# Zero products ahead of a recurrence moved from its own banks to the bank of the part before it, and two steps moved in a hand-written tail

## The chip, the cores and the metric

The kernel runs on one core of a Trainium2 chip. The metric is device time in microseconds (us) for one execution of the whole program. The engines are named as in the profile: PE (TensorE matmul), PEld (TensorE weight load), DVE (VectorE), ACT (ScalarE), POOL (GpSimd) and SP (SyncE, which only issues transfers here). ACTq and SPq are the issuing sides of ACT and SP.

## The reference, cut to what matters

The input is four images of 128 channels and 64 by 64 points. Two layers follow each other.

```python
# layer 0: layer norm over channels, a 3x3 depthwise convolution, attention in 16x16 windows
# layer 1, on t = the 4096 points of an image as tokens of 128 channels:
t = t + linear_attention(layer_norm(t))        # running sums of k v^T along the tokens
t = t + ffn(layer_norm(t))
# ffn: a recurrence along the tokens
Wx = batch_norm(x @ W.T)                       # mean and variance over ALL tokens of all images
y  = sigmoid(Wx[:, s] + y @ V.T)               # one step after another, s = 0, 1, 2, ...
```

The batch norm needs a mean and a variance over every token, so no step of the recurrence can use its input before the last token's product with W has been measured.

## The kernel before, in words

**First part.** The images are cut into 16 bands (`n` = 0 to 15) of 16 rows, and each band into four windows and into two halves of 512 tokens. The order of all instructions of PE, DVE, ACT and POOL is the order in which the Python code emits them: `in_order()` (line 249) chains each engine's instructions. What is emitted when is written out by hand in tables of step names: `START` for the first band, `SLOT` and `LAYER1` for the bands between, and `TAIL` (lines 83 to 95) for the end. A name like `product.z` is a step and the half that it works on. In `TAIL`, `y` and `z` are the two halves of band 14, `a` and `c` the two halves of band 15, the last one. `check.63` belongs to the last window (number 63).

The steps of layer 1 that matter here, each with its lines:

- `keep` (790): four PE transposes of the half's result (L313), an ACT copy to `rs_o` (L793), and a store of `rs_o` to memory from ACT's queue (L795).
- `measure_last` (680): four `bn_stats` and four `bn_aggr` on DVE (L292, L294), then two small POOL operations (L296, L297) that make 1/deviation for each token.
- `send` (683) and `spread` (694): SP writes these 512 factors to memory (L685), and ACT's queue reads them back to all 128 partitions as `factors` (L696, 256 KB).
- `product` (802): the product with W on PE (L815, two passes), then on DVE a multiplication with `factors` into `wx` (L816) and `bn_stats` of it (L822). The very last half, `c`, has no `factors`: it is normed first (`norm_last`, L304, and `turn_last`, four transposes L313 and an ACT copy L692), multiplied with W (L806), measured (L807), and then all statistics are combined: `bn_aggr` (L808), POOL's 1/deviation `sc` (L809, L810), `shift` (L811), and a copy of the product to `wx` (L812).
- `check` (606 and `in_range`, 550): three DVE operations that test whether the denominators of the attention lie in a range (L606, L554, L555).

The first part ends with `fill(bank(), 6)` (line 987). `fill(bk, n)` (267) issues `n` products of a constant zero matrix, 128x512 in bf16, to a PSUM bank. They compute nothing that is used.

**Recurrence.** All PSUM banks of the first part are given back (`main.close()`), and new ones are taken: two sets of three, `z0` to `z2`, and one called `okp`. One zero product goes to each of the six `z` banks (line 1053) and two to `okp`. Then come three products of the identity with `mv`, `sc` and `shift0` (L1057), whose results nobody reads. They wait for the statistics. Then the steps run: 4096 tokens of an image are cut into 128 segments of 32, all segments step together, and 9 steps (`WARM - 1`) at the end of the segments give the start values for the 32 counted ones. With one ACT step ahead of them, that makes 41 rounds. In each round, for three groups of columns, DVE has put `sc * wx + shift` into a `z` bank (`seed`, L1037, one operation for two rounds), PE adds `V y` to it (L1102), and ACT applies the sigmoid (L1107). POOL adds the residual (L1129), and the results are stored. The first round has a seed for itself alone; rounds 1 and 2 share the next three.

```python
def fill(bk, n):
    for _ in range(n):
        nc.tensor.matmul(bk, zeros, zeros[:, :1].to_broadcast([P, 512]), start=True, stop=True)
```

Of the kernel before, what the change touches and what calls it, by code (L numbers as in the profile page):

```python
# [17 lines left out]
P = 128  # L18
# [70 lines left out]
    "attend1.z keep.y send.y output.c spread.y measure.c turn.a measure_last.z",  # L89
    "norm.c keys.a values.a product.y queries.a turn.c turn_keys.a queries.c",  # L90
    "keys.c keep.z scores.a scores.c accumulate.a send.z attend0.a spread.z",
    "attend1.a check.63 values.c turn_keys.c measure_last.a send.a accumulate.c attend0.c",
    "attend1.c measure_last.c norm_last.c keep.a product.z spread.a product.a keep.c",
    "turn_last.c product.c",
)
DGROUP = 4
TINY, HUGE = 1e-30, 1e30
# [17 lines left out]
def conv_attn_hybrid(ctx: ExitStack, tc: tile.TileContext, ins: dict, out: bass.AP):  # L115
    nc = tc.nc
# [10 lines left out]
    def loaded(name, shape, dt=F32, src=None, eng=None):  # L127
# [4 lines left out]
    ident = const.tile([P, P], F32, name="ident")  # L132
# [12 lines left out]
        fill=0.0,  # L145
# [85 lines left out]
    for i in range(2):  # L231
        t = const.tile([P, 4, P + 1], F32, name=f"v1_{i}")
# [8 lines left out]
    shift0 = const.tile([P, 1], F32, name="shift0")  # L241
    beta0 = const.tile([P, 1], F32, name="beta0")
    mv = const.tile([P, 2], F32, name="mv")
    sc = const.tile([P, 1], F32, name="sc")
# [4 lines left out]
    def in_order():  # L249

        before = {}
        for ins in nc.cur_bb.bb.instructions[first:]:
            if ins.engine in ENGINES:
                if ins.engine in before:
                    tc.add_manual_dep(
                        ins,
                        before[ins.engine],
                        mybir.DependencyInfo(
                            mybir.DependencyClass.NoSync, mybir.DependencyReason.DATA
                        ),  # L260
                        reason="in order",
                    )
                before[ins.engine] = ins.name
# [3 lines left out]
    def fill(bk, n):  # L267

        for _ in range(n):
            nc.tensor.matmul(  # L270
                bk, zeros, zeros[:, :1].to_broadcast([P, 512]), start=True, stop=True
            )

    def bank():
        bk = ps.tile([P, 512], F32, tag="bank", name="bank")
        fill(bk, busy[0])
        busy[0] = 0
        return bk
# [569 lines left out]
    def do(what, which):  # L848
        name, at = what.split(".")
        if name == "warm":  # L850
            busy[0] += int(at)
            return
        h = which.get(at)
        if h is not None and name not in h.done:
            does[name](h)
            h.done.add(name)
# [125 lines left out]
    for what in " ".join(TAIL).split():  # L982
        if what.partition(".")[2].isdigit():
            block(what)
        else:
            do(what, which)
    fill(bank(), 6)
    in_order()
    main.close()

# [61 lines left out]
        for g in range(len(GROUPS)):  # L1052
            fill(ps_r.tile([P, 512], F32, tag=f"z{g}", name=f"z{g}"), 1)
    okp = ps_m.tile([P, 512], F32, tag="bank", name="bank")
    fill(okp, 2)
    for t in (mv[:, :1], sc, shift0):
        nc.tensor.matmul(  # L1057
            okp[:, :256], ident, t.to_broadcast([P, 256]), start=True, stop=True
        )


    warm = sp.tile([P, B, SEGS + 1], F32, name="warm")
    nc.gpsimd.memset(warm[:, :, 0:1], 0.0)

# [777 lines left out]
```

## Time and profile before

| what | value |
|---|---|
| median of 3 runs | 824.96 us (824.9 to 827.38) |
| the profiled execution's own time | 824.4 us |
| its span, first to last instruction | 822.6 us |
| mean granted TensorE clock over the span | 0.991 |
| PE busy | 795.0 us, 97% |
| DVE busy | 694.0 us, 84% |
| ACT busy | 530.2 us, 64% |
| POOL busy | 252.4 us, 31% |

The profiled execution lies 0.56 us under the median of the runs. Between its span and its time there are 1.8 us outside the instructions. Busy shares are averages over the whole program; the change touches only the stretch from about 749 us to 769 us, the seam between the two parts, so that stretch has to be read on its own: in order of time, with the wait that ends last before each step.

### The profile page before, as it was taken

What the parts mean: (1) busy time and instruction counts of PE and PEld (TensorE: products, weight loads), DVE (VectorE), ACT (ScalarE), POOL (GpSimd) and SP (SyncE); (2) the same over time, 40 slices, a digit from 0 to 9 for tenths busy, and PEclk for the clock granted to TensorE, in tenths of its full rate; (3) what the DMA queues carried; (4) which work ended last, traced back from release to release, by engine and by line L of the source; (5) the groups of instructions that cost most, each with busy time, mean ns of one, the idle gap of its engine ahead of it and who ended that gap; (6) DMA issues with size and microseconds to landing.
All of it is one profiled execution on the core that took longest, in us unless ns stands there. A gap on an engine that the chain in (4) does not pass through costs nothing.

```text
span 822.6 us, 28912 instructions
## 1 busy us (share of the span) xinstructions
PE 795.0 (97%) x11808; PEld 638.0 (78%) x11808; DVE 694.0 (84%) x2141; ACT 530.2 (64%) x1024; POOL 252.4 (31%) x362
## 2 busy tenths in 40 slices
PE   9999999999999999999999999999999999988893
PEld 6667878878787878788787878787887878766793
DVE  6657989998989898898979898998989896497885
ACT  4776566666767675766667676757666675622683
POOL 3023233413242332423132423323231312121193
PEclk9999999999999999999999999999999999999997
DMA  5122231414132232314132222323131312212796
GB/s 144 40 67 70 65 99 31 118 41 114 47 80 76 69 94 61 101 38 115 42 103 57 76 81 63 98 65 96 44 108 43 107 36 83 57 27 65 236 227 183
DMA packets 81430, 69.31 MB, mean 84 GB/s; under 512 B 44680, under 2 KB 63752, under 8 KB 81288
## 3 DMA queue, kind: packets, MB, share of 16 engines
q1 hardware_dynamic: 54072, 44.55, 19.1%
q10 hardware_dynamic: 26208, 19.15, 8.4%
q0 software_dynamic: 1008, 3.67, 2.6%
q8 instruction: 95, 1.56, 0.8%
q14 instruction: 47, 0.39, 0.2%
HBM read 40.03 MB, written 17.87 MB: 70 GB/s over the span
## 4 chain that ended last, share of the span: by engine, by line
PE 87%; DVE 6%; DMA 3%; POOL 1%; ACT 1%; issue 1%; SPq 0%; ACTq 0%; DVEq 0%; POOLq 0%
PE bank L483 13%; PE bank L536 7%; PE bank L565 7%; PE bank L654 7%; PE bank L701 7%; PE bank L496 6%; PE bank L580 6%; PE bank L313 5%; PE z L1102 5%; PE bank L717 3%; PE bank L738 3%; PE bank L815 3%; PE bank L755 3%; PE bank L774 3%; PE bank L776 3%; PE bank L523 3%
## 5 line engine op out<-in xcount | busy, mean ns | idle before, releaser
L421 DVE SCALAR_TENSOR_TENSOR y<-ypad,cpe_w,y 128x512 f32<-128x512 f32 x240 | 184.6, 769 | 12.1 <-ACT y L419 7.6
L545 ACT ACTIVATE es<-bank 128x512 f32<-128x512 f32 x256 | 132.2, 603 | 33.5 <-PE bank L536 33.5
L296 POOL TENSOR_SCALAR rs<-mv 128x4 f32<-128x4 f32 (+2 forms) x99 | 25.3, 256 | 371.4 <-DVE mv L294 369.7
L628 POOL TENSOR_TENSOR oT<-o_sb,rden 128x512 f32<-128x512 f32 x63 | 81.3, 1290 | 114.5 <-DMA rden<-rd 85.6
L297 POOL TENSOR_TENSOR rs<-rs,mhalf 128x4 f32<-128x4 f32 (+2 forms) x99 | 105.3, 1064 | 8.3
L580 PEld LDWEIGHTS bank<-es,v_sb 128*32 128x32 f32 x3072 | 63.2, 110 | 36.7 <-issue 32.2
L491 ACT COPY k<-bank 128x512 f32<-128x512 f32 x64 | 38.6, 603 | 64.3 <-PE bank L483 64.3
L536 PEld LDWEIGHTS bank<-q,k 32*64 32x64 f32 x4096 | 75.4, 130 | 2.7
L536 PE MATMUL bank<-q,k 32*64 32x96 f32 (+1 forms) x4096 | 77.5, 274 | 0.0
L565 PE MATMUL bank<-es,ones 128*32 128x512 f32 x512 | 71.2, 605 | 0.0
L580 PE MATMUL bank<-es,v_sb 128*32 128x96 f32 (+1 forms) x3072 | 70.0, 237 | 0.0
L654 PEld LDWEIGHTS bank<-woT,oT 128*128 128x128 f32 x512 | 59.5, 192 | 12.3 <-POOL oT L628 8.5
L483 PE MATMUL bank<-y2w,wqT 128*128 128x256 f32 x256 | 66.2, 381 | 0.0
L568 ACT COPY den<-bank 128x512 f32<-128x512 f32 x64 | 37.3, 583 | 44.7 <-PE bank L565 42.4
L483 PE MATMUL bank<-y2w,wkT 128*128 128x256 f32 x256 | 66.1, 381 | 0.0
L496 PE MATMUL bank<-wvT,y2w 128*128 128x256 f32 x256 | 65.9, 380 | 0.0
L701 PE MATMUL bank<-xl,awT 128*128 128x512 f32 x128 | 63.2, 594 | 1.8 <-ACT xl L678 1.8
L654 PE MATMUL bank<-woT,oT 128*128 128x128 f32 x512 | 60.6, 276 | 4.5 <-POOL oT L628 4.5
L703 ACT ACTIVATE low<-bank,minus 128x512 f32<-128x512 f32 x64 | 44.0, 687 | 22.4 <-PE bank L701 20.9
L292 DVE BATCH_NORM_STATS2 st<-x 128x6 f32<-128x128 f32 x256 | 55.4, 279 | 0.6
L496 PEld LDWEIGHTS bank<-wvT,y2w 128*128 128x128 f32 x256 | 48.5, 190 | 7.5 <-DVE y L421 0.8
L611 DVE TENSOR_TENSOR dc<-dc,pad_c 128x32 f32<-128x32 f32 x63 | 22.3, 353 | 37.5 <-DMA dc<-den 37.2
(151 smaller groups left out, 1673.2 us busy)
## 6 DMA issues: line engine op xcount, KB each, us to landing
rden<-rd SPq DMA_DIRECT2D x63, 256.0 KB
v_sb<-v_sb SPq DMA_DIRECT2D x128, 64.0 KB
factors<-factors ACTq DMA_DIRECT2D x31, 256.0 KB
xin<-in_xt SPq DMA_DIRECT2D x15, 512.0 KB
out<-rs_o ACTq DMA_DIRECT2D x16, 256.0 KB
resd<-rs_o ACTq DMA_DIRECT2D x16, 256.0 KB
out<-ot SPq DMA_DIRECT2D x32, 128.0 KB
out<-ys POOLq DMA_DIRECT2D x7, 512.0 KB, 6.9
```

Of the source, the lines that this page charges most:

```text
L292: nc.vector.bn_stats(st[:, j, :], piece)
L297: nc.gpsimd.tensor_tensor(rs[:, :n], rs[:, :n], mhalf[:, :n], ALU.pow)
L421: nc.vector.scalar_tensor_tensor(y2, src, cpe_w[:, tap : tap + 1], y2, ALU.mult, ALU.add)
L483: nc.tensor.matmul(pps[:, br * WT : (br + 1) * WT], wT[:, br * P : (br + 1) * P], y2, start=True, stop=True,)
L496: nc.tensor.matmul(vps[:, e * 256 : (e + 1) * 256], y2[:, e * P : (e + 1) * P], wvT, start=True, stop=True,)
L536: nc.tensor.matmul(sps[h][half * KC : (half + 1) * KC, cols], w["k"][rows, k0 : k0 + KC], w["q"][rows, cols], start=False, stop=br == BR - ...
L545: nc.scalar.activation(es, sps[h], AF.Exp, scale=scale)
L565: nc.tensor.matmul(dps[rows], ones[:, :HD], w["es", h], start=True, stop=True)
L580: nc.tensor.matmul(ops[rows, cols], w["v"][:, n, c0 : c0 + HD], w["es", h][:, cols], start=(br, n) == pieces[0], stop=(br, n) == pieces[-1],)
L628: nc.gpsimd.tensor_tensor(oTs[n][:, :, :, wj * WS : (wj + 1) * WS], w["o"].rearrange("p (a r c) -> p a r c", a=BR, c=WS), w["rden"].rearra ...
L654: nc.tensor.matmul(yps[:, j * P : (j + 1) * P], oT[:, br, t], woT[:, br, :], start=br == 0, stop=br == BR - 1,)
L701: nc.tensor.matmul(zps, awT[:, m * P : (m + 1) * P], h.xl, start=True, stop=True)
```

## The change

The zero products at the end of the first part go from 6 to 20. The two zero products to `okp` and the three products of the identity are dropped, the six to the `z` banks stay. In the tail, `check.63` goes from behind `attend1.a` to a place just ahead of `product.c`, and `product.z` goes from behind `keep.a` to a place ahead of `norm_last.c` and `keep.a`. On PE, `product.z` so stands ahead of the four transposes of `keep.a`; on DVE it stands ahead of the four L304 of `norm_last.c`. The order of the transfers on SP's and ACT's queues is as before.

```diff
     "attend1.z keep.y send.y output.c spread.y measure.c turn.a measure_last.z",
     "norm.c keys.a values.a product.y queries.a turn.c turn_keys.a queries.c",
     "keys.c keep.z scores.a scores.c accumulate.a send.z attend0.a spread.z",
-    "attend1.a check.63 values.c turn_keys.c measure_last.a send.a accumulate.c attend0.c",
-    "attend1.c measure_last.c norm_last.c keep.a product.z spread.a product.a keep.c",
-    "turn_last.c product.c",
+    "attend1.a values.c turn_keys.c measure_last.a send.a accumulate.c attend0.c attend1.c",
+    "measure_last.c product.z norm_last.c keep.a spread.a product.a keep.c turn_last.c",
+    "check.63 product.c",
 )
...
-    fill(bank(), 6)
+    fill(bank(), 20)
     in_order()
     main.close()
...
     okp = ps_m.tile([P, 512], F32, tag="bank", name="bank")
-    fill(okp, 2)
-    for t in (mv[:, :1], sc, shift0):
-        nc.tensor.matmul(
-            okp[:, :256], ident, t.to_broadcast([P, 256]), start=True, stop=True
-        )
```

## The prediction

> **What bounds the kernel now.** I read the clock row of the page first, then the chain of waits in order of time, then the seam in short stretches, then the instructions in order of time. PE is busy for 97% of the span, but around 764 us the chain passes through products that compute nothing:
>
> ```profile
> 760.53 0.69 DVE stats L822
> 761.22 0.61 DVE stats L807
> 761.83 0.02 issue
> 761.85 1.03 DVE mv L808
> ...
> 763.06 0.61 DVE wx L812
> 763.67 0.05 issue
> 763.72 2.34 PE z L270 x6
> 766.06 0.85 PE bank L270 x2
> 766.91 1.69 PE bank L1057 x6
> 768.61 38.79 PE z L1102 x242
> ```
>
> Columns: start, length, what. DVE leads up to 763.67, the statistics of the last half. Then eleven products without use fill PE until the recurrence. The next view has busy time by engine in two stretches; the third number from the end is PE's granted clock:
>
> ```profile
> 761.40:763.70 2.30, 0.00 (x0) 0.00 (x0) 2.19 (x4) 1.49 (x2) 0.65 (x2) 1.00 0.59 181
> 764.20:767.60 3.40, 3.40 (x10) 1.76 (x9) 3.05 (x8) 1.37 (x3) 0.00 (x0) 0.50 1.06 354
> ```
>
> PE is idle for 2.3 us, waiting for L812, and then has half its clock for 3.4 us. In order of time the recurrence's other needs are there sooner:
>
> ```profile
> 755.20 0.33 ACTq L696 DMA_DIRECT2D factors<-factors  x1
> 756.78 1.11 DVE L304 TENSOR_SCALAR xn<-x,mv,rs 128x128 f32<-128x128 f32 x4 [1.41 <-POOL rs L297]
> ...
> 759.48 1.01 DVE L816 TENSOR_TENSOR wx<-bank,factors 128x512 f32<-128x512 f32 x1
> 759.92 1.47 PE L270 MATMUL bank<-zeros 128*128 128x512 bf16 x6
> ...
> 764.28 1.37 ACT L1079 ACTIVATE ys<-wx,shift,sc 128x176 f32<-128x176 f32 x3 [0.59 <-DVE shift L1018]
> 764.64 2.78 DVE L1037 TENSOR_SCALAR z<-wx,sc,shift 128x176 f32<-128x176 f32 x6
> 768.45 3.81 PE L1102 MATMUL z<-ys,fvT 128*128 128x176 f32 x23
> ```
>
> The first `ys` exists at about 764.8 and the first seed at 765.1; the first L1102 runs at 768.45. So 3.3 us of PE's queue lie bare. Before that, DVE's only pause is the 1.41 us at 756.78.
>
> [...]
>
> **The change part by part**, in the times of the profiled execution.
>
> *check.63 leaves its place.* It costs 0.69 us on DVE (749.37 to 750.06 in the chain). `measure_last.a` and so `send.a` come 0.69 earlier. The next DVE step (L763) needs PE's L755, which starts only at 750.31, and L784 at 752.41 follows PE's L776; so `measure_last.c` still ends at 755.4. Gain there: about 0. What hides it is PE, and it leaves 0.6 us of DVE idle.
>
> *product.z goes first.* On DVE its L816 and L822 (1.05 and 0.63 to the next start) run in the pause: 755.40 to 757.08 instead of waiting until 756.78. L304 starts 0.3 late, at 757.08, and with it `turn_last`, L806 and the first zero product (759.92 to 760.22). L304 would free DVE at 758.16.
>
> On PE its two passes (0.43 each) now delay the transposes of `keep.a` from 753.10 to 753.96. Behind these stand, on ACT's queue, the copy L793 (753.74 to 754.60), the store L795 (754.35 to 755.21) and, 0.35 later, the broadcast L696: issue at 755.56 instead of 755.20. Before, L696 waited for `send.a`; that now lands 0.69 sooner and no longer decides.
>
> *The broadcast is late next.* How long it takes must be bounded. That of `z` was issued at 744.51, 0.42 behind a store, and the DMA share falls to 0 at 748.25: 3.7 us, and a completion some tenths later. That of `a`, 0.85 behind a store, had its data by 759.0, at most 3.8. Now it follows its store by 0.35. I take 4.0 to the wait's end (3.5 to 4.6): 759.6 (759.1 to 760.2). DVE is free at 758.16, so `product.a` waits 1.4 us, a new wait, and starts 0.15 later than before (759.48).
>
> Queued behind it on DVE: `check.63` (0.69, no longer hidden), then L807. So L807 goes from 761.14 to 759.63 + 1.66 + 0.69 = 762.0, that is 0.86 later. L808, `sc`, `shift0` and L812 follow: L812 ends at 764.53. The `res` loads on SP, ACT and POOL's memset, which waited for the last L816, now wait for `check.63` (about 1.5 us later). ACT then issues two loads and the table load, some 3.2 us as before, and is ready for L1079 at 765.3. The loads ended at 776 (DMA share) and would now end near 777.5; POOL's first read of `res`, at 779.10 before and near 777.5 then, needs only the first half of them, so I cost this at nothing.
>
> *20 zero products, not 6.* They run from 760.22 every 0.218 us, to 764.58, and bridge the idle 2.3 us. The clock stays full[...]. The six `z` products follow L812 without a gap, until 765.9 instead of 766.06.
>
> *Five products dropped.* Off the path: 0.85 + 1.69 = 2.54 us at the clock that they had.
>
> *The recurrence.* Seeds start at 764.64 + 0.86 = 765.50; `z` bank 0 is ready by then. The first is seen by PE about 0.5 later, so L1102 starts at 766.1. But the six seeds take 2.78 us, to 768.28; round 1's last group needs the sixth. Before, it ran 1.56 us after the first L1102 (770.01 against 768.45). 768.40 - 1.56 = 766.84 is where the recurrence effectively starts. The rounds, 38.8 us, and the end stay as they are.
>
> **Sum:** 768.45 - 766.84 = 1.6 us less. The profiled execution gives 824.4 - 1.6 = 822.8; the median shown stands 0.56 above it, so 824.96 - 1.6 = **823.4 us**, 0.19% less. About 0.3% (2.5 us) is what a measurement of this kernel can tell from no change, so I call this no change.
>
> **Rivals.**
>
> *Faster: broadcast in time, seeds hidden.* If the broadcast lands by 759.0, L807 is 0.2 later, and seeds allow 766.2; if the sixth seed costs nothing, PE's own queue sets 765.9. 768.45 - 765.9 = 2.55, so 822.4; a few tenths less where the runs have further half-clock windows. For it: other broadcasts ended within 3.8 us. Against: six seeds back to back on DVE.
>
> *No half clock before.* [...]in some executions the old seam may keep its clock. Its eleven products then end near 766.8 and the change gains -0.1: 825.0. Against: the profiled run has the half clock and is the quickest of the times shown.
>
> *Slower: the broadcast waits behind stores.* `check.63` and L807 stand behind it. Each 0.1 us of lateness costs 0.1. Break-even is a landing at 761.2, 5.6 us after issue; at 764 the time is 827.8. For it: the stores of `keep.a` and `keep.c` move 0.86 and 0.75 later[...]. Against: no such time to landing in the trace.
>
> *The clock falls anyway.* If a half-clock window meets the 20 products, they end up to 1.7 later (824.9). Against: the longest pauses ahead of them are 0.7 each.
>
> **Numbers.** No change 0.58 (my sum 0.40, no half clock 0.12, clock falls 0.06), faster by over 0.3% 0.33, slower by over 0.3% 0.09. The likeliest case alone, with the bounds of the broadcast, is 822.8 to 824.0. The range for 8 in 10 reaches into the faster and the unthrottled case: 821.6 to 825.4.
>
> **What would show it.** Right: clock 1.00 from 755 to 768; L807 near 762.0 with DVE idle ahead of L816 on a DMA; six `z` products without a pause; L1102 near 766.1 with waits for DVE in round 1. Wrong: L816 of `product.a` straight behind L304; PE idle ahead of the `z` products; a half-clock stretch; or the recurrence longer than 39.5 us.

## The result, and the profile after

The changed kernel was timed against the kernel before twice, each time with runs of both in one comparison. The medians were 825.2 us (22 runs) against 825.52 us (22 runs), a ratio of 0.9998 with a 95% interval of 0.9986 to 1.001; and, with the variants below, 824.55 us (22 runs) against 824.81 us (67 runs), a ratio of 0.9981, interval 0.9967 to 0.9996. The mean of the two ratios is 0.9990, or 0.9 us of 825; the two intervals allow 0.1 to 1.6 us for that mean when their errors are taken as independent (half widths 0.0012 and 0.0015, together 0.0009). By the bound of 0.3% that is no change, as forecast. Single runs of one kernel lie up to 8 us apart (820.12 to 828.07 for the kernel before), so that every statement on a microsecond needs many runs.

The profiled execution took 823.65 us, its span 821.9 us. To compare traces I measure one stretch in each: from the first L755 of `accumulate.c` (750.31 before, 751.84 after) to the first sigmoid of the recurrence's third round. I call it the **seam**. It took 20.57 us before and takes **18.57 us** after. From there to the start of PE's last product the two traces have 37.74 and 37.75 us. The profile after took only 0.75 us less, because its seam starts 1.5 us later; ahead of the seam it has a stretch at half clock, from 63.15 to 66.57 us, which the profile before has not.

The lines of the recurrence stand 7 lower than before: L1095 is the old L1102. This is the chain of waits after, in order of time (start, length, what):

```profile
756.90 0.93 DVE wx L816
...
757.86 0.69 DVE stats L822
758.55 0.26 DVE xn L304
...
759.98 0.59 ACT xl L692
...
760.62 1.12 PE bank L806 x2
761.75 0.22 PE bank L270
...
762.02 4.09 PE bank L270 x18
...
766.16 1.46 PE z L270 x6
767.62 0.87 PE z L1095 x6
```

Before, this chain ran on DVE from 756.78 on, over both L816 and the statistics, to the end of L812 at 763.67. Now it leaves DVE with L304 and stays on PE but for one copy: L806, the zero products in the old bank, the zero products in the `z` banks, the recurrence. The path through the statistics has vanished from it. In order of time, with each wait in brackets:

```profile
757.15 0.39 ACTq L696 DMA_DIRECT2D factors<-factors  x1
...
760.33 1.04 DVE L816 TENSOR_TENSOR wx<-bank,factors 128x512 f32<-128x512 f32 x1 [0.77 <-DMA factors<-factors]
...
762.70 0.69 DVE L807 BATCH_NORM_STATS2 stats<-bank 128x6 f32<-128x512 f32 x1
...
764.55 0.68 DVE L812 COPY wx<-bank 128x512 f32<-128x512 f32 x1
...
766.63 4.94 DVE L1037 TENSOR_SCALAR z<-wx,sc,shift 128x176 f32<-128x176 f32 x10 [0.55 <-PE z L270]
767.46 3.73 PE L1095 MATMUL z<-ys,fvT 128*128 128x176 f32 x19
```

Two waits are new. `product.a` waits 0.77 us for the broadcast, as forecast. And the first seed (L1037) waits 0.55 us for the zero product in its `z` bank, where it started 0.14 us behind the operation ahead of it before: L812 ends at 765.23, but PE reaches the `z` banks only at 766.16, 0.93 later. At the 0.218 us from one to the next that this trace shows, twenty zero products are too many by about four. Busy time by engine in two stretches (third number from the end: granted clock):

```profile
759.50:766.10 6.60, 5.87 (x23) 2.48 (x24) 5.39 (x14) 2.19 (x4) 0.86 (x3) 1.00 0.35 104
766.20:767.60 1.40, 1.40 (x7) 0.77 (x7) 0.97 (x3) 1.04 (x3) 0.00 (x0) 1.00 1.05 367
```

The clock is full and PE has no pause of 2.3 us. So the profile shows 2.0 us gone, and the timed runs only about half of that. The experiments ask which edit brought what, what bounds the new seam, and where the rest went.

### The profile page after: what moved, and what is told of

The parts are those of the page before. It is cut to its first block, busy times and chain, and to the rows that moved or that the text cites. A ratio compares the mean times of both kernels' runs of the same rounds, so it can differ in the third digit from the quotient of the medians.

```text
span 821.9 us, 28920 instructions
## 1 busy us (share of the span) xinstructions
PE 796.2 (97%) x11811; PEld 638.9 (78%) x11814; DVE 698.0 (85%) x2141; ACT 530.2 (65%) x1024; POOL 253.2 (31%) x362
## 4 chain that ended last, share of the span: by engine, by line
PE 93%; DVE 3%; ACT 1%; DMA 1%; POOL 1%; issue 0%; SPq 0%; DVEq 0%; POOLq 0%
PE bank L483 14%; PE bank L565 8%; PE bank L536 8%; PE bank L654 7%; PE bank L580 7%; PE bank L496 7%; PE bank L701 7%; PE bank L313 6%; PE z L1095 5%; PE bank L717 3%; PE bank L755 3%; PE bank L774 3%; PE bank L738 3%; PE bank L776 3%; PE bank L815 3%; PE bank L523 3%
## 5 line engine op out<-in xcount | busy, mean ns | idle before, releaser
L580 PEld LDWEIGHTS bank<-es,v_sb 128*32 128x32 f32 x3072 | 63.2, 110 | 36.7 <-issue 32.2
L654 PEld LDWEIGHTS bank<-woT,oT 128*128 128x128 f32 x512 | 61.2, 196 | 12.2 <-POOL oT L628 8.5
L654 PE MATMUL bank<-woT,oT 128*128 128x128 f32 x512 | 62.2, 280 | 4.5 <-POOL oT L628 4.5
L701 PE MATMUL bank<-xl,awT 128*128 128x512 f32 x128 | 63.2, 594 | 2.0 <-ACT xl L678 2.0
L611 DVE TENSOR_TENSOR dc<-dc,pad_c 128x32 f32<-128x32 f32 x63 | 25.5, 405 | 33.3 <-DMA dc<-den 33.2
```

What stands on the lines that cost most here:

```text
L580: nc.tensor.matmul(ops[rows, cols], w["v"][:, n, c0 : c0 + HD], w["es", h][:, cols], start=(br, n) == pieces[0], stop=(br, n) == pieces[-1],)
L654: nc.tensor.matmul(yps[:, j * P : (j + 1) * P], oT[:, br, t], woT[:, br, :], start=br == 0, stop=br == BR - 1,)
L701: nc.tensor.matmul(zps, awT[:, m * P : (m + 1) * P], h.xl, start=True, stop=True)
```

## Experiments

Theory A was the profile's: the seam is 2.0 us shorter in every run. Its rivals came as the results did: B, the added products or the moved tail eat the gain; C, the half clock does not meet the old seam in every run; D, PE's 20 products bind the new seam, and DVE does not. All kernels were timed in rounds beside the kernel before.

| kernel | seam in its profile, us | half clock in the seam, us after its start | ratio to before | 95% interval |
|---|---|---|---|---|
| before | 20.57 | 13.9 | | |
| before, again (e1) | 20.59 | 14.6 | 0.9997 | 0.9983 to 1.0012 |
| five products dropped (e2) | 18.11 | 8.1 | 0.9970 | 0.9958 to 0.9981 |
| 20 zero products (e3) | 19.67 | none | 0.9994 | 0.9976 to 1.0012 |
| tail moved (e4) | 20.61 | 14.7 | 0.9989 | 0.9977 to 1.0001 |
| changed kernel | 18.57 | none | 0.9998 | 0.9986 to 1.001 |
| changed kernel, again (e8) | 18.58 | none | 0.9981 | 0.9967 to 0.9996 |
| e2 and 20 products (e9) | 20.05 | 8.6 | 0.9988 | 0.9973 to 1.0004 |
| e2 and the tail (e10) | 18.39 | 9.0 | 0.9992 | 0.9974 to 1.001 |
| e2, new order, 13 products (e6) | 17.47 | none | 0.9968 | 0.9954 to 0.9983 |
| no zero product (e7) | 21.17 | 11.2, for 6.83 us | 1.0019 | 1.0005 to 1.0032 |
| 10 zero products (e11) | 18.90 | none | 0.9993 | 0.9979 to 1.0008 |
| changed, check.63 back (e12) | 18.57 | none | 0.9991 | 0.9978 to 1.0005 |
| changed, 14 products (e13) | 18.95 | 9.1 | 0.9987 | 0.9972 to 1.0002 |

**The three edits one by one.** e1 is the unchanged kernel.

> The kernel before, unchanged, timed against itself. Seam here means: from the start of the last L755 (accumulate.c) to the start of the third round's first sigmoid. In the profile before it was 770.89 - 750.31 = 20.6 us with a half-clock stretch inside, after it 770.41 - 751.84 = 18.6 without. My theory (the gain is there where the seam of before has its half clock, and the half-clock stretches elsewhere scatter the times): the seam is 20.6 if its idle 2.3 us meets a half clock and about 18.9 (20.6 - 1.7) if not, and the comparison with itself has a scatter of some 1 us in the median, which is as much as the gain looked for. Rival (the change has a loss of its own that eats a steady 2 us gain): the seam is 20.6 in each execution and the times of equal kernels agree within 0.1%.

Measured: 0.9997, and the seam repeats to 0.02 us. This is what the comparison cannot tell apart.

e2 drops only the five products:

```diff
-    fill(okp, 2)
-    for t in (mv[:, :1], sc, shift0):
-        nc.tensor.matmul(
-            okp[:, :256], ident, t.to_broadcast([P, 256]), start=True, stop=True
-        )
```

> Only the five products without use ahead of the recurrence are dropped; 6 zero products and the old tail. My theory: the seeds then bound the start, 764.64 + 3.78 = 768.4 for the third round's first sigmoid, so a seam of 18.1 at full clock and up to 18.8 with the half-clock stretch: 0.8 to 1.8 us less than before, nearly all that the whole change brings. Rival (the 20 zero products bring the gain by the clock): the seam stays near 20 us.

Measured: 0.9970, 2.5 us less, more than the whole change gives. The chain of waits of e2 (its L1097 is the old L1102), and busy time in its half clock:

```profile
764.46 0.61 DVE wx L812
765.12 1.48 PE z L270 x6
766.60 0.96 PE z L1097 x4
```

```profile
759.85:763.15 3.30, 2.58 (x4) 1.04 (x6) 3.23 (x5) 0.45 (x1) 0.10 (x1) 0.50 0.04 14
```

A half clock does meet this seam, at 8.1 us. But PE has only six zero products there and then waits for L812 anyway, so they take the wait's time and the seam is 18.11 all the same.

e3 changes only the count, e4 only the order of the tail (both as in the diff above):

```diff
-    fill(bank(), 6)
+    fill(bank(), 20)
```

> Only the zero products at the end of the first part go from 6 to 20; the five products and the old tail stay. My theory: full clock, the six z products from 764.3, the five others until 767.3, so a seam of 19.5 in every execution: 1.1 less than a before with half clock and 0.6 more than one without; no difference in the median within 1 us. Rival (the clock is the gain): 1.7 us less in the median.

> Only the tail is moved as in the change; 6 zero products and the five others stay. My theory: the pause at L304 that product.z fills is paid back by the later broadcast and by check.63 behind it, L807 stands 10.9 us after L755 as in both profiles (761.14 - 750.31 = 10.8, 762.70 - 751.84 = 10.9), the seam is 20.6 with the half clock or 18.9 without, no difference. Rival (a loss in the tail eats the gain of the rest): L807 comes 0.5 us or more later, and the time is 1 to 2 us longer.

Measured: e3 keeps its clock and has a seam of 19.67, 0.9 less than before; in time, 0.9994. e4 leaves the seam as it was (20.61), and its L807 stands 10.84 us after the seam's start, 10.83 before: what `product.z` gives in DVE's pause, `check.63` takes back. Its 0.9989 has an interval that reaches to no change, and nothing in the seam stands behind it. So, of the three edits, the dropping alone makes the seam shorter than the changed kernel has it.

**The changed kernel again, and in pairs of edits.**

> The changed kernel once more, timed against the kernel before beside its own variants. The stretch from the start of accumulate.c's L755 to the third round's first sigmoid was 20.57 us before and 18.57 after in the two profiles, and the dropping of five products alone gave 2.5 us of time. Theory A (the 2.0 us of the stretch are real in the timed runs; the first comparison, 0.17 us with an interval of 1 us to either side, met them with half-clock windows elsewhere): about 823.4, a ratio of 0.9975. Theory B (the moved tail and the 20 products cost in the timed runs what the dropped products give, by a half clock that the profile happened to miss): 825.2, a ratio of 1.000, and a half clock or a later L1095 in the stretch of this profile.

Measured: seam 18.58, time 0.9981: the ratio of theory A lies within this interval, and its seam is as in the first profile. Theory B's later L1095 is not there. With the first comparison, though, A's 2.0 us are not reached.

e9 is e2 with 20 zero products, e10 is e2 with the moved tail.

> Five products dropped and 20 zero products, the tail as before. By the prediction's steps the moved tail costs 0.86 us (check.63 uncovered ahead of L807): without it the zero products run from 759.92 to 764.28, L812 ends at 763.67, the sixth seed 0.86 earlier, so the stretch is 18.57 - 0.86 = 17.7 us if seeds bind, 18.1 if PE's 26 products bind. Theory A (the profile's: L807 stood at 10.86 after, 10.83 before, so the tail costs nothing): 18.1 to 18.5, no half clock in the stretch, time 822.9 to 823.4. Theory B (the tail is what eats the gain): 822.5 or less, at least 1.5 us below the changed kernel beside it.

> Five products dropped and the tail moved, 6 zero products as before. Theory A: PE is idle from 761.7 to about 764.5, 2.8 us, so most runs have the half clock over the six z products and the first round: the stretch is 18.6 us where the window misses it, 19.5 to 20.3 where it meets it; time 823.4 to 824.6. Theory B (the 20 products eat the gain): as fast as the dropping alone, 823.1.

Both profiles caught the early half clock. e9's busy time in it, and its chain:

```profile
763.10:766.40 3.30, 3.03 (x5) 1.20 (x7) 3.23 (x5) 0.00 (x0) 0.10 (x1) 0.50 0.00 0
```

```profile
765.87 4.39 PE bank L270 x18
770.30 1.46 PE z L270 x6
```

In order of time, e9's last copy of the statistics:

```profile
767.17 0.68 DVE L812 COPY wx<-bank 128x512 f32<-128x512 f32 x1
```

L806 (2.07 us, 1.12 in the changed kernel) and the first zero products run at half clock, the 20 start late and still run, and PE comes to the `z` banks at 770.30, 2.45 us after L812 has ended (767.85). The seam is 20.05, where I had expected 18.1 to 18.5. In e10, with six zero products, the same half clock (at 9.0 us) costs little: seam 18.39, with L812 0.24 later than in the changed kernel and 0.28 later than in e2. So the added products turn a half clock that cost nothing into one that costs up to 2 us (20.05 against the 18.11 of e2, one profile each). That is theory B's mechanism, in some executions. The times do not show it: e9 and e10 cannot be told from the changed kernel, and e10, without added products, is no nearer to e2 than e9. Its median, 823.9 us, lies where theory A had it (823.4 to 824.6), not at B's 823.1, but its interval reaches both.

**What binds the new seam.** e12 puts `check.63` back behind `attend1.a` and changes nothing else; e13 cuts the zero products of the changed kernel from 20 to 14.

> The changed kernel with check.63 back behind attend1.a alone (product.z stays first, 20 zero products). By the prediction's steps check.63 costs 0.69 behind product.a and nothing at its old place: L807 at 10.2 us after accumulate.c's L755 (10.86 after), L812 at 12.0. Theory D (in the changed kernel PE's 20 zero products bind, to 14.3, since the second seed there waited 0.55 for a z product): L1095 still at 15.6, the third round at 18.4 to 18.57, no gain from DVE's 0.69. Theory of the prediction (DVE's statistics and seeds bind): 17.9.

> The changed kernel with 14 zero products instead of 20. Theory D (PE's zero products bind and the seeds wait for the z products): 14 end at 12.8, L812 at 13.4, z products 13.45 to 14.8, first L1095 at 14.9, the third round at first seed + 3.88 = 18.16, 0.4 less than after; the pause is 0.6 us, no half clock; time 0.4 us less than the changed kernel. Theory of the prediction (20 products end with L812, so that fewer of them give nothing): 18.57 as after.

In e12, L807 stands at 10.37 instead of 10.86 us (0.49 earlier; `product.a` waits longer for its broadcast), L812 0.50 earlier, and the seam is 18.57, unchanged. In order of time:

```profile
765.28 0.68 DVE L812 COPY wx<-bank 128x512 f32<-128x512 f32 x1
...
767.39 1.46 PE L270 MATMUL z<-zeros 128*128 128x512 bf16 x6
767.87 3.33 DVE L1037 TENSOR_SCALAR z<-wx,sc,shift 128x176 f32<-128x176 f32 x7 [1.06 <-PE z L270]
```

All that DVE gained is waited away at the first seed: 1.06 us for its `z` bank, 0.55 in the changed kernel. (The expectation calls it the second seed.) Theory D is shown: PE's zero products bind, because they hold up the first seed. e13 did not give its answer: the early half clock met it at 9.1 us, its 14 products ended at 766.1, and the seam was 18.95, not 18.16. The 18.16 was not seen in a profile; the time (0.9987) agrees with it and with 18.57.

e6 frees both: five products dropped, 13 zero products, and this order.

```diff
-    "attend1.a values.c turn_keys.c measure_last.a send.a accumulate.c attend0.c attend1.c",
-    "measure_last.c product.z norm_last.c keep.a spread.a product.a keep.c turn_last.c",
-    "check.63 product.c",
+    "attend1.a check.63 values.c turn_keys.c measure_last.a send.a accumulate.c attend0.c",
+    "attend1.c measure_last.c keep.a product.z norm_last.c spread.a product.a keep.c",
+    "turn_last.c product.c",
-    fill(bank(), 20)
+    fill(bank(), 13)
```

> Five products dropped, 13 zero products, check.63 back behind attend1.a (hidden by PE there), and product.z in DVE's pause but behind keep.a's transposes, so that the broadcast isn't late. By the prediction's steps this keeps the 0.74 us that product.z's place gives and loses none: L807 at 10.1 us after accumulate.c's L755 (10.83 before, 10.86 after), L812 at 11.95, seeds from 13.5, PE's z products from about 12.1 to 13.4; the stretch 17.8 us at full clock, 0.7 less than after. Theory A: 822.7. Rival: PE decides, not DVE (keep.a's transposes ahead of product.z delay L816 or the first zero product), and the stretch is 18.5 as after.

Measured: L807 at 10.19, seam 17.47, 0.3 less than expected, and 0.9968 in time, the best of all, level with e2. Only the broadcast came late all the same: it was issued 4.80 us after the seam's start, and `product.a` waited for it until 8.51. Its chain of waits, and the start of its seeds in order of time:

```profile
762.35 2.57 PE bank L270 x11
...
764.96 1.46 PE z L270 x6
766.42 0.95 PE z L1095 x4
...
767.40 0.33 ACT ys L1100
```

```profile
765.50 0.22 DVE L1019 SCALAR_TENSOR_TENSOR shift<-shift,sc,beta 128x1 f32<-128x1 f32 x1
...
765.85 5.49 DVE L1037 TENSOR_SCALAR z<-wx,sc,shift 128x176 f32<-128x176 f32 x11
```

The first seed follows L1019 without a wait for a `z` bank: the products no longer hold it up. From the start of the first seed to the third round it is 3.77 or 3.78 us in all eight profiles of kernels with the five products dropped: e6 (13.69 to 17.47), e2 (14.34 to 18.11) and e10 (14.62 to 18.39), where the seed does not wait, but also the changed kernel (14.79 to 18.57). So DVE's six seeds set this last stretch in each, and zero products cost what they delay the first seed by. In the changed kernel DVE was ready for it at about 14.38, as soon after L1019 as before; the surplus costs it 0.4 us.

**How often the old seam met the half clock.** e11 and e7 change only the count of zero products in the kernel before, to 10 and to 0.

> The kernel before with 10 zero products instead of 6: they end before L812, so nothing is delayed, and the pause falls from 2.3 to about 1.4 us[...]. So this is the kernel before with its eleven products at full clock: the z products and five more end at about 16.2 us after accumulate.c's L755, first L1102 there, third round at 18.8 (20.57 with the half clock). Theory C (about half of the runs of before had the half clock): 1.0 us faster than before, ratio 0.9988. Theory A (all had it): 1.8 us faster, ratio 0.9978.

> The kernel before with no zero product at the first part's end instead of 6: PE's pause ahead of the z products grows from 2.3 to 3.8 us, and nothing else moves. [...] The half clock costs the stretch about 1.8 us. Theory C (the half clock meets the old seam in about half of the runs only, so the change gains half of what its profile shows): this kernel is 0.6 to 0.9 us slower than before, ratio 1.0009, mean clock 0.0005 to 0.001 lower. Theory A (it meets every run of before): no difference, ratio 1.000. Stretch from accumulate.c's L755 to the third round in the profile: 20.6 to 21.0 with the half clock.

e11's busy time in the pause and after it, and its chain:

```profile
762.60:763.60 1.00, 0.00 (x0) 0.00 (x0) 0.96 (x3) 0.99 (x2) 0.54 (x2) 1.00 0.85 252
763.80:767.00 3.20, 3.20 (x16) 2.17 (x17) 2.95 (x9) 1.37 (x3) 0.01 (x1) 1.00 1.05 353
```

```profile
763.07 0.61 DVE wx L812
763.73 1.48 PE z L270 x6
765.21 0.43 PE bank L270 x2
765.64 1.30 PE bank L1057 x6
766.94 8.08 PE z L1102 x50
```

This is the old seam with its eleven products at full clock: 3.2 us for them instead of 4.9, seam 18.90. So the half clock cost the old seam 1.67 us, and without it the changed kernel is only 0.33 shorter (18.57). The time of e11 was 0.9993: 0.6 us less. Theory C's 0.9988 lies within the interval, theory A's 0.9978 just outside; with the 1.67 us measured, A asks 0.9980, just inside. e2's 2.5 us (interval 1.6 to 3.5) is what A asks of its seam (2.46). e7 was slower by 1.6 us (0.4 to 2.6), which A's "no difference" excludes; but its profile was at half clock for 6.83 us where before was for 3.41, and its seam is 0.6 us longer, which A could have allowed for. Against C stands, too, that all four profiles of kernels with the old seam's pause (before, e1, e4, e7) met the half clock, and that the mean granted clock of e11's timed runs was 0.9931, 0.0024 above that of the runs beside it; 3.41 us at half clock in every run would be 0.0021 by my estimate (half of 3.41, of a span of 823). (Between e1 and the runs of the same kernel beside it that mean differs by 0.0009.) The times leave the share open.

The traces show that equal instructions need not meet it alike. At 63 us, where the two kernels have the same instructions, PE waits for `oT` ahead of L654, 2.77 us in the profile after and 2.92 before; after, it was then at half clock from 63.15 to 66.57, before it kept its clock. In the seam, before and e1, one kernel, have the half clock from 13.9 and from 14.6 us on. The changed kernel and e13 have the same pauses of PE ahead of their zero products, 0.53 us ahead of the last L313 group and 0.68 ahead of L806; e13 met the half clock there, the changed kernel did not. So theory C is possible; in what share of the runs the half clock comes was not measured.

What share the times ask is an estimate from the seams. Let p be the share of the runs of before with the half clock, and q that of the changed kernel with the early one. The gain is then 0.33 + 1.67 p - 1.5 q (18.90 against 18.57; 20.57 against 18.90; 20.05, which is e9's, against 18.57). The 0.9 us measured asks p = 0.34 where q is 0, and q = 0.73 where p is 1. e11 (0.6 us) asks p = 0.36, e2 (2.5 us, of which 0.79 without any half clock before: 18.90 against 18.11) asks p = 1.0, and their intervals have about 0.5 to 1.0 in common. It is an estimate, not a proof of C.

## Why the prediction was right or wrong

The forecast of no change held, and the 825.2 us of the first comparison lie in the range, 1.8 above the predicted 823.4. By the prediction's own steps:

- **check.63 off its place gives nothing, PE hides it.** Right: in the trace after, DVE stands idle for 0.64 us at L763, waiting for L755; the forecast was 0.6.
- **product.z in the pause, L304 0.3 later, first zero product 0.3 later.** Right in kind, half in size: counted from the seam's start, the first L304 stands at 6.63 (6.47 before, 6.77 forecast), the first zero product at 9.75 (9.61 before, 9.91 forecast). Before, `product.z`'s last product ended at about 755.5, and its L816 ran at 757.82, behind L304, which waited until 756.78. That is what the change filled the pause with.
- **The broadcast is issued 0.36 later and decides over product.a.** Right in kind: issued at 5.31 (forecast 5.25), and L816 waits for the DMA. **The term that was mis-sized is its time to landing:** 4.0 us taken, with 3.5 to 4.6 as bounds; 3.2 measured (757.15 to 760.33), outside them. It is no constant: 4.1 for the broadcast of `z` before (issued 744.51, its data over at 748.32, landed at 748.61), 3.2 to 3.4 in the six profiles with this tail or e12's, 3.7 in e6; what sets it stays open. So in the changed kernel L816 started at 8.49 rather than at 9.3, and check.63 behind it cost nothing net: L807 at 10.86, where 11.69 was forecast and 10.83 was before.
- **20 zero products end with L812.** They ran 0.218 us apart and ended when forecast (`z` products from 14.32; forecast 14.27). But L812 ended 0.8 earlier than forecast, at 13.39, so the products bind instead of being cover. e12 shows it. That the products ended within 0.1 us of where the forecast had the end of L812 (14.22) is luck, and so is it that the start of the recurrence came out near. The rival "broadcast in time" had this: PE's own queue sets the start then. It put the first L1102 at 15.59 (measured 15.62), but took the seeds as hidden.
- **Five products off the path, seeds stall round 1 by 0.74.** The first L1095 came at 15.62 (forecast 15.79). The first two intervals between the rounds' first sigmoids exceed the steady 0.97 by 0.51 together. The seam so lost 2.0 us where 1.6 was summed: the difference is 0.17 from the first L1095 and 0.23 from the stall.
- **No half clock before (chance 0.12).** Under-weighted, if theory C holds in part: e11 puts the old seam at full clock at 18.90, a gain of 0.33 for those runs (forecast -0.1). The reason given against it was one profile with the half clock, which does not say how often; the estimate above has such runs between none (e2) and about two thirds (e11).
- **The clock falls anyway (chance 0.06).** Under-weighted, and its argument failed: "the longest pauses ahead of them are 0.7 each" did not keep the clock (e13 met the half clock behind pauses of 0.53 and 0.68). The half clock started 8.1 to 9.1 us into the seam in four of fourteen profiles (e2, e9, e10, e13), two of them with the changed tail (e10 with 6 zero products, e13 with 14). In the changed kernel itself it was not caught; that it costs there what it costs e9 is argued, and how often it comes there was not measured.

So the sum was near for the profiled executions, and too high for the mean of the runs. For the missing 1.1 us (2.0 in the trace, 0.9 in time) two causes are left, both with a size from an experiment: runs of before without half clock, which lose 1.67 of the 2.0, and runs of the changed kernel with the early one, where up to 1.5 (20.05 against 18.57) go back. By the estimate the first alone would do with 0.66 of the runs of before, the second alone with 0.73 of those of the changed kernel. No run measured the parts, and the scatter of the runs (0.1 to 1.6 us for the gain) is as large.

## What to carry to other kernels

Products without use that bridge a pause are themselves on the path as soon as the clock halves or their consumer comes early: count them to end a little before the consumer's operand, and drop products between operand and consumer first; dropping five alone gave 2.5 us (1.6 to 3.5), dropping them with 20 zero products in e9 1.0 (-0.3 to 2.2), intervals that overlap, while the traces show the cost of the surplus. One profile with a half clock, or without, does not speak for every run: here the changed kernel and e13 have the same pauses, 0.53 and 0.68 us, and in their profiles only e13 met it. So price both cases, with it and without it, for the kernel before and for the changed one. A wait taken off one queue is worth something only until the next queue's turn, so ask, for the early end of each bound as well as for the late one, what decides then.

## What the runs showed of the hardware

The half clock in the seams lasted 3.41 us (before: 764.17 to 767.58), in e7 6.83. In it one zero product (128x512, bf16) started 0.427 us after the other (before), at full clock 0.218 us (after). The two passes of L806 took 1.12 us at full clock (after), and 1.84 (e13) and 2.07 us (e9) where the half clock met them.

I had not expected how little idleness there is ahead of it. Before, it came 0.45 us after the end of a pause of PE of 2.3 us; in e13 the pauses in the 4 us ahead of it were 0.68 us at most. Nor does a pause always bring it: before, a pause of 2.92 us ended at 62.88, and the clock was full from 63.2 to 66.5. In ten of the fourteen profiles a stretch at about 63 us was at half clock, in four it was not. The scatter of the runs goes with it: the seam starts at 749.3 to 750.3 us in the four profiles without it and at 751.5 to 754.5 us in the ten with it. What decides on the clock was not shown.
